# The tail of a fused conditioning and ternary-FFN kernel: gelu and last quarter by halves, a new order of the last matmuls, and second units at other pairs

## The chip, the core and the metric

The kernel runs on one core of a Trainium2 chip. The metric is device time in microseconds (us): 963.6 us is the median of four runs before the change (963.25 to 963.78). One more execution was recorded by the hardware profiler. It took 963.3 us, its span from the first to the last instruction is 961.5 us, and every time "at" some microsecond below counts from the start of that span. The engines are PE (TensorE, matmuls; PEld is its weight load), DVE (VectorE), ACT (ScalarE), POOL (GpSimd) and SP (SyncE, which only issues DMAs here).

## What is computed

Cut to what matters, the reference is

```python
w = weights[conditions]                      # one 64x64 matrix for each of 128 samples
c = einsum('bct,bcd->bdt', x, w)             # x: 128 x 64 x 512
h = gelu(c @ ternarize(W1).T + b1)           # 512 -> 2048
y = h @ ternarize(W2).T + b2                 # 2048 -> 512
scale = max(abs(y)) / 7 + 1e-8               # one scale for the whole tensor
out = x + clip(round(y / scale), -7, 7) * scale
```

ternarize replaces a weight matrix by alpha times a matrix of -1, 0 and 1.

## The kernel before, in words

The samples are worked in 16 blocks (n = 0 to 15) of 8 samples, which is 4 pairs of samples or 512 rows of 512 numbers. The hidden dimension is worked in 16 chunks (hc = 0 to 15) of 128. Every float32 activation is carried as two parts: a high part (k = 0, float32r) and a low part (k = 1, float16, what the high part lost). A chunk's hidden values are computed by layer 1, go through gelu, are split into the two parts, and layer 2 then adds their products with W2 into four accumulators `ypsum[n][j]`, j = 0 to 3, one for each quarter of the block's 512 rows, 128 x 512 float32, one PSUM bank each. The profile calls these accumulators py.

From block 2 on, chunks are worked in pairs by `pair(n, k)` and `seven(n, k, ...)`, k = 0 to 7: chunks 2k and 2k + 1 come out of seven products instead of eight. The products land in the PSUM tiles xy and z; ACT copies and DVE adds gather them into two SBUF tiles ha and hb (the profile calls these ring or x_quarters). Then come, for each of the two chunks, gelu (`gelu7`, ACT), a scaling copy that makes the high part (`high7`, with `up`, ACT; the profile's h) and the low part (`low`, with `rest`, DVE; the profile's low_parts or low_last). Layer 2 runs one pair behind: the matmuls of pair k use the chunks of pair k - 1 (`before[0]`, `before[1]`). POOL casts the fp8 weights to float32r for the high parts: `widen7` for the seven products (buffers `w1f[0..3]`), `widen2` for layer 2 (buffers `w2f[hc % 2]`); the profile calls all of them wf. Low parts use the fp8 weights directly (w1t, w2t, sums).

In the last block the low-part matmuls of chunks 8 to 15 (`HELD` = 8) are held back until all pairs are done. They and the last chunks' high parts make the tail at the end of the listing, a list of (quarter j, chunk hc, part k) that is worked in order. After a quarter's last matmul come y (DVE: accumulator times alpha plus bias), quantization (ACT), the largest magnitude (DVE, ymax) and `last_x(j)` (DVE: x plus quantized y times the scale, then the store). After the last quarter `widened` and `largest_of` form the maximum over the last blocks.

The quantization of earlier blocks must not wait for the end. Blocks 0 to 11 give a known maximum, from which the scale is taken; at the very end the maximum of the other blocks (top_rest) is compared with it, and a branch redoes the output if it is larger. So during blocks 12 to 15 finished half-blocks, "units", are put out between the pairs: `next_steps` quantizes a unit (ACT), `next_out` adds x (DVE) and stores it (SP), one unit behind the quantization. After every second unit `ahead_x` loads the x (and for blocks 0 and 1 the kept y) of a block to come; the load of the last block's x is the last of these. A pair has one unit (at `behind(0)`) or none; at some pairs a second unit is put in, quantized at `behind(2)` and added at `behind(4)`. The line `second = ...` in `pair` says which: in the last block, pairs 0 and 3.

What sets the order: each engine runs its instructions in the order in which the program text issues them (`InOrder` keeps that order), and waits only where data or buffers ask for it. `seven` calls `behind(i)` at fixed places between its products, and `behind` puts in what belongs there (casts, units, gathers, results of the block before). In `seven`, `last` is true only for pair 7 of block 15; there the order of the gelus and scalings already differs: gelu and scaling of the first chunk stand ahead of the second chunk's. The results of a block (y out of the accumulators) are taken at the end of pair 0 and the start of pair 1 of the next block.

The profile puts nearly everything on line 36, the helper that issues, so instructions are told apart by their tiles.

Of the kernel before, what the change touches and what calls it, by code (L numbers as in the profile page):

```python
# [15 lines left out]
AF = mybir.ActivationFunctionType  # L16
ALU = mybir.AluOpType
AX = mybir.AxisListType
# [21 lines left out]
def tile_cond_ternary_ffn(  # L40
# [51 lines left out]
    def pair_of_pairs(h):  # L92
        return slice(h * PAIRS // 2, (h + 1) * PAIRS // 2)
# [155 lines left out]
    def flat(w):  # L249
        return w.rearrange("p a b -> p (a b)")  # L250
# [129 lines left out]
    def widen2(n, hc):  # L380
        if n == 0 and hc < NH - LAG:
            w = w2f[hc % 4]
        else:
            w = w2f[hc % 2]
        if n == 0:
            g, i = divmod(hc, GH)
            pool.tensor_copy(w, group1(terns2, g)[:, i * T : (i + 1) * T])
        else:
            pool.tensor_copy(w, w2t[:, hc])
        wide2[n, hc] = w  # L390
# [44 lines left out]
    def two_of(n, hc):  # L435

        if not low_parts:
            t = half.tile([P, 4, BLK], F16, tag="half", name="low_parts")
            low_parts.extend(t[:, i, :] for i in range(4))
        if n == NB - 1 and hc == HELD:  # L440
            t = big.tile([P, NH - HELD, BLK], F16, tag="big", name="low_last")
            low_parts[:] = [t[:, i, :] for i in range(NH - HELD)]
        high = quarter.tile([P, BLK], F32R, tag="quarter", name=f"h_{n}_{hc}")
        return high, low_parts[hc % len(low_parts)]
# [3 lines left out]
    def up(high, h):  # L448
        act.activation(high, h, AF.Copy, scale=UP)

    def rest(two, h):
        dve.scalar_tensor_tensor(two[1], h, UP, two[0], ALU.mult, ALU.subtract)

    def low(n, hc):

        open_low.pop((n, hc), lambda: None)()

    def layer2(n, hc, js=range(PAIRS), ks=(1, 0), ends=None):
        two = hidden[n, hc]
        w = wide2[n, hc], wide2[n, hc] if n == 0 else w2t[:, hc]  # L460
        begins, ends = ks[0], ks[-1] if ends is None else ends
        if n not in ypsum:
            ypsum[n] = [
                ps_y.tile([P, T], F32, tag=f"py{j}", name=f"py{j}_{n}") for j in range(PAIRS)
            ]
        for k in ks:
            for j in js:
                pe.matmul(
                    out=ypsum[n][j],
                    lhsT=two[k][:, j * P : (j + 1) * P],  # L470
                    rhs=w[k],
                    start=(hc == 0 and k == begins and ends != begins),
                    stop=(hc == NH - 1 and k == ends),
                    skip_group_check=True,
                )
# [176 lines left out]
    def behind(hc):  # L652
        if hc == 6:
            largest2(0)
        if 6 <= hc < 6 + NG - 1:
            largest2(hc - 5)
        if hc == 7:
            sign1(3)
        if hc == 8:
            signed1(3)  # L660
        if hc == 11:
            delta.extend(next(find))
            signed2(0)
        if hc == 12:
            for i in (1, 3):
                low(0, i)
            signed2(1)
        if hc in (13, 14):
            widen2(0, hc - 13)
# [135 lines left out]
    def seven(n, k, behind, before, last):  # L805

        xb, xt, xl = cond[n]
        b11, b21, b22 = [(xb[:, i : i + 2], xl[:, i : i + 2]) for i in (0, 2, 4)]
        t1, t2, t3, t4 = [(xt[:, i : i + 2], xl[:, i + 6 : i + 8]) for i in (0, 2, 4, 6)]
        x, y = extra["xy"] if k % 2 == 0 else extra["xy"][::-1]  # L810
        x, y = x[:, :HALF], y[:, :HALF]
        z = extra["z"]
        p4, p5 = z[:, :HALF], z[:, HALF:]

        def both(w, narrow):
            return w, narrow.rearrange("p (c h) -> p c h", c=2)

        s0, s1, s2, s3 = sums_of(k)
        w11, w12 = both(w1f[0][:, :2], a11[:, k]), both(w1f[0][:, 2:], a12[:, k])
        w22 = both(w1f[1][:, 2:], a22[:, k])  # L820
        u0, u1 = both(w1f[1][:, :2], s0), both(w1f[2][:, :2], s1)
        u2, u3 = both(w1f[2][:, 2:], s2), both(w1f[3][:, :2], s3)

        def tokens(t):

            return t.rearrange("p (j h d) -> p h j d", j=PAIRS, h=2)

        def turned(t):
            return t.rearrange("p (j d) -> p j d", j=PAIRS)

        def gelu7(i, h):
            act.activation(h, h, AF.Gelu, bias=b1t[:, 2 * k + i : 2 * k + i + 1], scale=alpha[1])

        def high7(i, h):
            hc = 2 * k + i
            hidden[n, hc] = two = two_of(n, hc)
            up(two[0], h)
            open_low[n, hc] = lambda: rest(two, h)

        ha, hb = hf[0], hf[1]  # L840
        if n == NB - 1 and k % 2 == 1:
            ha, hb = extra["x"][:, 0, :], extra["x"][:, 1, :]
        ha_2, hb_2 = tokens(ha), tokens(hb)
        behind(0)
        product(x, w11, b11, 0, first=True)
        product(p5, u0, t1, 0, first=True)
        product(p4, w22, t4, 0)
        product(x, w11, b11, 1, last=True)
        act.copy(ha_2[:, 0], turned(x))
        product(p5, u0, t1, 1, last=True)  # L850
        product(p4, w22, t4, 1, last=True)
        act.copy(hb_2, z.rearrange("p (h j d) -> p h j d", h=2, j=PAIRS))
        behind(1)
        product(y, w12, b21, 1, first=True)
        product(y, w12, b21, 0, last=True)
        dve.tensor_tensor(ha_2[:, 0], turned(y), ha_2[:, 0], ALU.add)
        product(x, u1, t2, 0)
        product(x, u1, t2, 1, last=True)
        act.copy(ha_2[:, 1], turned(x))
        behind(2)  # L860
        product(p5, u2, b22, 1)
        product(p5, u2, b22, 0, last=True)
        dve.tensor_tensor(ha_2[:, 1], turned(p5), ha_2[:, 1], ALU.add)
        behind(3)
        layer2(*before[0], (0, 1), (0,), ends=1)
        product(x, u3, t3, 0)
        product(x, u3, t3, 1, last=True)
        dve.tensor_tensor(
            hb_2, turned(x).unsqueeze(1).to_broadcast([P, 2, PAIRS, C]), hb_2, ALU.add
        )  # L870
        gelu7(0, ha)
        behind(4)
        if last:
            high7(0, ha)
            gelu7(1, hb)
        else:
            gelu7(1, hb)
            high7(0, ha)
        if n < NB - 1 or before[0][1] < HELD:
            layer2(*before[0], (0, 1), (1,), ends=1)  # L880
            layer2(*before[0], (2, 3), (1,), ends=0)
            layer2(*before[1], ks=(1,), ends=0)
        layer2(*before[0], (2, 3), (0,), ends=0)
        layer2(*before[1], ks=(0,), ends=0)
        high7(1, hb)
        for i in range(2):
            low(n, 2 * k + i)
        behind(6)
# [128 lines left out]
    def widened(top, name):  # L1017

        top1 = const.tile([P, 1], F32, name=f"top1_{name}")
        dve.tensor_reduce(top1, top.rearrange("p n j -> p (n j)"), AX.X, ALU.max)  # L1020
        dve.tensor_copy(ones_f, top1.to_broadcast([P, P]))
        return ones_f
# [6 lines left out]
    def pair(n, k):  # L1029
# [11 lines left out]
        def behind(i):  # L1041
            if i == 0 and n >= KNOWN:
                if n == KNOWN and k < 2:
                    fetch_x(order[k])
                if k != 1 and (n > KNOWN or k > PAIRS - 1) and not (final and k > LAST):
                    next_steps()
                    next_out(True)
            second = n >= KNOWN and k in ((0, 3) if final else (0, NH // 2 - 1) if n > KNOWN else (NH // 2 - 1,))
            if i == 3 and n == KNOWN and k == PAIRS - 1:
                largest_of(tops_known.pop(), top_known, ps_c, "pc")  # L1050
                steps_of(scale, inverse, top_known)
# [80 lines left out]
    assert done[1] == len(units)  # L1132
    widen2(*steps[-1])
    pool.drain()
    lows = [(hc, 1) for hc in range(HELD, NH - 1)]
    rest_of = [(NH - 2, 0), (NH - 1, 0), (NH - 1, 1)]
    whole = lows + [(NH - 1, 1), (NH - 1, 0), (NH - 2, 0)]
    tail = [(0, *t) for t in lows + rest_of] + [(1, *t) for t in whole]
    tail += [(2, *t) for t in whole[::-1]] + [(3, *t) for t in whole]
    for i, (j, hc, k) in enumerate(tail):  # L1140
        final = all(j != t[0] for t in tail[i + 1 :])
        layer2(n, hc, [j], (k,), k if final else 1 - k)
        if not final:
            continue
        y = last[:, j, :]
        dve.scalar_tensor_tensor(y, ypsum[n][j], alpha[3], b2b, ALU.mult, ALU.add)
        act.activation(quant[:, j, :], y, AF.Identity, scale=inverse)
        dve.tensor_reduce(
            ymax[:, n, j : j + 1], y, AX.X, ALU.max, apply_absolute_value=True
        )  # L1150
        if j == PAIRS - 1:
            wide = widened(ymax[:, KNOWN:], "rest")
        last_x(j)
    top_rest = const.tile([P, 1], F32, name="top_rest")
    largest_of(wide, top_rest, ps_h, "ph")
# [74 lines left out]
```

## Time and profile before

| what | value |
|---|---|
| median of 4 runs | 963.6 us (963.25 to 963.78) |
| the profiled execution | 963.3 us, span 961.5 us |
| PE busy | 950.1 us, 99% of the span |
| DVE, POOL, ACT busy | 708.6, 706.3, 637.0 us |
| last pair's first product | 940.58 us |
| the six layer-2 matmuls at the end of the last pair | from 944.24 us |
| first matmul of the tail's list | 945.70 us |
| first y of the tail | 948.18 us |
| end of PE's last layer-2 matmul | 954.7 us |
| start of the last add of x | 956.82 us |
| end of the final comparison | 957.96 us |

The page of a profile begins with busy times of the engines and ends with groups of instructions; the groups give engine, operation, output and inputs by name, shapes, count, busy time, mean duration of one in ns, and after a bar the idle time of the engine just before them with what ended it. The chain follows the work that ended last back to the start: start, duration, engine and tile. A timeline row gives start, duration, engine, operation and, in brackets, the idle time before it. Instructions of one engine can overlap a little, so the distance between two starts is often shorter than a duration; a matmul of 512 columns has a row of about 0.4 us but follows the one before it by about 0.22 us.

### The profile page before, as it was taken

How to read it: one execution, taken by the hardware profiler on the slowest of the kernel's cores; microseconds unless marked ns; L12 is line 12 of the kernel's file. 1: busy time of each engine (PE TensorE's matmuls, PEld its weight loads, DVE VectorE, ACT ScalarE, POOL GpSimd, SP SyncE). 2: the span in 40 equal slices, each digit the busy share in tenths (PEclk: the TensorE clock that was granted, in tenths of full speed). 3: DMA queues.
4: the chain of work that ended last, by engine and by line, in shares of the span. 5: the costliest groups of instructions: out<-in, count | busy, mean ns of one | idle time of the engine just before them, and what ended most of it. 6: DMA issues, size and time to landing. Idle time of an engine off the chain costs nothing.

```text
span 961.5 us, 17574 instructions
## 1 busy us (share of the span) xinstructions
PE 950.1 (99%) x6072; PEld 739.5 (77%) x6072; DVE 708.6 (74%) x1239; ACT 637.0 (66%) x1148; POOL 706.3 (73%) x1060
## 2 busy tenths in 40 slices
PE   8999999999999999999999999999999999999997
PEld 4687667888788788788878778788878878878784
DVE  7999766666676766666676676666667798888986
ACT  7995445656656666665666656666565777878784
POOL 5866867677686776767767686776767879788872
PEclk9999999999999999999999999999999999999999
DMA  9201011110111100111020111100131184574751
GB/s 358 104 23 47 14 33 49 28 66 15 35 49 34 59 25 25 50 43 49 25 70 15 34 50 33 59 23 27 49 121 60 46 301 177 184 244 165 279 203 61
DMA packets 33195, 80.11 MB, mean 83 GB/s; under 512 B 3792, under 2 KB 3792, under 8 KB 30160
## 3 DMA queue, kind: packets, MB, share of 16 engines
q1 hardware_dynamic: 31056, 76.86, 22.9%
q0 software_dynamic: 2048, 2.10, 0.8%
q8 instruction: 49, 0.80, 0.4%
q14 instruction: 42, 0.34, 0.1%
HBM read 46.44 MB, written 32.51 MB: 82 GB/s over the span
## 4 chain that ended last, share of the span: by engine, by line
PE 96%; POOL 1%; DVE 1%; DMA 1%; issue 0%; ACT 0%; ACTq 0%; POOLq 0%
PE py L36 47%; PE xy L36 22%; PE z L36 16%; PE ph L36 6%; PE pc L36 6%; POOL wg L36 1%; DMA wg<-in_L_cond_weights,rows 1%; DVE xt L36 0%; DVE y_last L36 0%; POOL wf L36 0%; ACT diag L36 0%; DMA first<-in_itok_B 0%; POOL diag L36 0%; PE number L36 0%; DVE y L36 0%
## 5 line engine op out<-in xcount | busy, mean ns | idle before, releaser
L36 PE MATMUL py<-wf,h 128*128 128x512 f32 x1088 | 316.5, 416 | 0.7 <-DVE y L36 0.6
L36 POOL CAST wf<-w2t 128x512 fp32r<-128x512 fp8e4 x240 | 230.0, 979 | 105.2 <-PE py L36 102.2
L36 POOL CAST wf<-sums 128x256 fp32r<-128x256 fp8e4 (+1 forms) x336 | 183.2, 551 | 86.0 <-PE xy L36 82.4
L36 DVE SCALAR_TENSOR_TENSOR low_parts<-ring,h 128x512 f16<-128x512 f32 x228 | 202.5, 926 | 39.3 <-ACT h L36 39.3
L36 PEld LDWEIGHTS py<-wf,h 128*128 128x128 f32 x1088 | 196.6, 189 | 45.1 <-POOL wf L36 0.8
L36 PE MATMUL py<-w2t,low_parts 128*128 128x512 fp8e4 x920 | 218.6, 379 | 0.0
L36 ACT ACTIVATE ring<-ring,b1t,alpha_up 128x512 f32<-128x512 f32 x216 | 175.2, 818 | 58.8 <-DVE ring L36 53.9
L36 DVE TENSOR_TENSOR ring<-xy,ring 128x256 f32<-128x256 f32 x216 | 119.8, 555 | 119.2 <-PE xy L36 119.2
L36 ACT COPY ring<-xy 128x256 f32<-128x256 f32 x216 | 80.5, 373 | 171.6 <-PE xy L36 171.1
L36 PEld LDWEIGHTS <-low_parts 128*128 128x128 f16 x920 | 89.7, 98 | 84.4 <-issue 0.3
L36 ACT ACTIVATE h<-ring 128x512 fp32r<-128x512 f32 x232 | 133.9, 626 | 0.6
L36 POOL CAST wf<-w1t 128x256 fp32r<-128x256 fp8e4 (+1 forms) x240 | 131.3, 563 | 2.5 <-PE xy L36 0.3
L36 PE MATMUL xy<-xb,wf 128*128 128x256 f32 x448 | 98.8, 302 | 0.0
L36 PE MATMUL xy<-xt,wf 128*128 128x256 f32 x448 | 88.1, 277 | 0.1
L36 PE MATMUL xy<-xl,sums 128*128 128x256 f16 x448 | 87.9, 278 | 0.0
L36 PE MATMUL xy<-xl,w1t 128*128 128x256 f16 x448 | 86.8, 275 | 0.0
L36 PE MATMUL z<-xl,sums 128*128 128x256 f16 x448 | 85.6, 273 | 0.0
L36 PEld LDWEIGHTS xy<-xt,wf 128*128 128x128 f32 x448 | 76.2, 188 | 10.2 <-issue 0.2
L36 PEld LDWEIGHTS xy<-xb,wf 128*128 128x128 f32 x448 | 75.9, 189 | 10.2
L36 PEld LDWEIGHTS <-sums 128*128 128x128 fp8e4 x896 | 69.3, 97 | 14.7
L36 POOL DMA_INDIRECT wg<-in_L_cond_weights,rows x64 | 64.0, 999 | 18.2 <-issue 8.6
L36 PEld LDWEIGHTS <-w1t 128*128 128x128 fp8e4 x736 | 61.6, 98 | 18.0 <-issue 4.3
(134 smaller groups left out, 1349.7 us busy)
## 6 DMA issues: line engine op xcount, KB each, us to landing
xt<-in_x SPq DMA_DIRECT2D x36, 512.0 KB
y_dram<-y SPq DMA_DIRECT2D x15, 1024.0 KB
out<-xt SPq DMA_DIRECT2D x30, 512.0 KB
x_quarters<-in_x SPq DMA_DIRECT2D x56, 256.0 KB
nat<-in_L_ffn_W SPq DMA_DIRECT2D x6, 1024.0 KB
y_back<-y_dram SPq DMA_DIRECT2D x2, 1024.0 KB
nat<-in_L_ffn_W SPq DMA_DIRECT2D x3, 512.0 KB
wg<-in_L_cond_weights,rows POOLq DMA_INDIRECT x64, 2.5
```

What stands on the lines that cost most here:

```text
L36: return lambda *args, **kw: self._tc.keep_in_program_order(make(*args, **kw))
```

## The change

There are four edits.

1. In the last pair of the last block (`last` in `seven`), the add that completes hb is made in two halves of its columns, and gelu, scaling and low part of the second chunk are made for 256 columns at a time. The function then returns: the six layer-2 matmuls that stood at its end (chunk 12 for quarters 2 and 3, chunk 13 for all four) move into the tail.
2. The tail's list has a new order. Quarter 0 comes first, with the low parts of chunks 8 to 13 in front, then 13 high, 14 high, 14 low, 15 high, 15 low. Quarters 1 and 2 follow with 11 and 12 matmuls. Quarter 3 is worked in two column halves of its output: 12 matmuls of 256 columns, then y, quantization and maximum of these 256 columns, then the same for the other 256. The last add of x still takes all 512 columns. The second half's maximum goes into a slot of ymax that belongs to block 11, and the final reduction reads 20 values instead of 16.
3. `widen2` puts the last two chunks' weights into `w1f[0]` and `w1f[1]`, since the buffers `w2f` now stay in use until the tail.
4. In the last block the second units stand at pairs 3 and 4 instead of pairs 0 and 3.

```diff
--- before.py
+++ after.py
@@ -380,6 +380,8 @@
     def widen2(n, hc):
         if n == 0 and hc < NH - LAG:
             w = w2f[hc % 4]
+        elif n == NB - 1 and hc >= NH - 2:
+            w = flat(w1f[hc - NH + 2])
         else:
             w = w2f[hc % 2]
         if n == 0:
@@ -455,7 +457,7 @@
 
         open_low.pop((n, hc), lambda: None)()
 
-    def layer2(n, hc, js=range(PAIRS), ks=(1, 0), ends=None):
+    def layer2(n, hc, js=range(PAIRS), ks=(1, 0), ends=None, cols=slice(0, T)):
         two = hidden[n, hc]
         w = wide2[n, hc], wide2[n, hc] if n == 0 else w2t[:, hc]
         begins, ends = ks[0], ks[-1] if ends is None else ends
@@ -466,9 +468,9 @@
         for k in ks:
             for j in js:
                 pe.matmul(
-                    out=ypsum[n][j],
+                    out=ypsum[n][j][:, cols],
                     lhsT=two[k][:, j * P : (j + 1) * P],
-                    rhs=w[k],
+                    rhs=w[k][:, cols],
                     start=(hc == 0 and k == begins and ends != begins),
                     stop=(hc == NH - 1 and k == ends),
                     skip_group_check=True,
@@ -865,17 +867,24 @@
         layer2(*before[0], (0, 1), (0,), ends=1)
         product(x, u3, t3, 0)
         product(x, u3, t3, 1, last=True)
-        dve.tensor_tensor(
-            hb_2, turned(x).unsqueeze(1).to_broadcast([P, 2, PAIRS, C]), hb_2, ALU.add
-        )
+        for js in [pair_of_pairs(h) for h in range(2)] if last else [slice(0, PAIRS)]:
+            t = hb_2[:, :, js]
+            added = turned(x)[:, js].unsqueeze(1).to_broadcast(list(t.shape))
+            dve.tensor_tensor(t, added, t, ALU.add)
         gelu7(0, ha)
         behind(4)
         if last:
             high7(0, ha)
-            gelu7(1, hb)
-        else:
-            gelu7(1, hb)
-            high7(0, ha)
+            low(n, 2 * k)
+            hidden[n, 2 * k + 1] = two = two_of(n, 2 * k + 1)
+            for part in halves:
+                gelu7(1, hb[:, part])
+                up(two[0][:, part], hb[:, part])
+                rest([t[:, part] for t in two], hb[:, part])
+            behind(6)
+            return
+        gelu7(1, hb)
+        high7(0, ha)
         if n < NB - 1 or before[0][1] < HELD:
             layer2(*before[0], (0, 1), (1,), ends=1)
             layer2(*before[0], (2, 3), (1,), ends=0)
@@ -1045,7 +1054,7 @@
                 if k != 1 and (n > KNOWN or k > PAIRS - 1) and not (final and k > LAST):
                     next_steps()
                     next_out(True)
-            second = n >= KNOWN and k in ((0, 3) if final else (0, NH // 2 - 1) if n > KNOWN else (NH // 2 - 1,))
+            second = n >= KNOWN and k in ((3, 4) if final else (0, NH // 2 - 1) if n > KNOWN else (NH // 2 - 1,))
             if i == 3 and n == KNOWN and k == PAIRS - 1:
                 largest_of(tops_known.pop(), top_known, ps_c, "pc")
                 steps_of(scale, inverse, top_known)
@@ -1132,24 +1141,30 @@
     assert done[1] == len(units)
     widen2(*steps[-1])
     pool.drain()
-    lows = [(hc, 1) for hc in range(HELD, NH - 1)]
-    rest_of = [(NH - 2, 0), (NH - 1, 0), (NH - 1, 1)]
-    whole = lows + [(NH - 1, 1), (NH - 1, 0), (NH - 2, 0)]
-    tail = [(0, *t) for t in lows + rest_of] + [(1, *t) for t in whole]
-    tail += [(2, *t) for t in whole[::-1]] + [(3, *t) for t in whole]
-    for i, (j, hc, k) in enumerate(tail):
-        final = all(j != t[0] for t in tail[i + 1 :])
-        layer2(n, hc, [j], (k,), k if final else 1 - k)
-        if not final:
-            continue
-        y = last[:, j, :]
-        dve.scalar_tensor_tensor(y, ypsum[n][j], alpha[3], b2b, ALU.mult, ALU.add)
-        act.activation(quant[:, j, :], y, AF.Identity, scale=inverse)
-        dve.tensor_reduce(
-            ymax[:, n, j : j + 1], y, AX.X, ALU.max, apply_absolute_value=True
-        )
+    a, b, c, d = range(NH - 4, NH)
+    lows = [(hc, 1) for hc in range(HELD, b + 1)]
+    tail = [(0, *t) for t in lows + [(b, 0), (c, 0), (c, 1), (d, 0), (d, 1)]]
+    tail += [(1, *t) for t in [(d, 1), (c, 1)] + lows + [(b, 0), (c, 0), (d, 0)]]
+    tail += [(2, *t) for t in [(d, 0), (c, 0), (b, 0), (a, 0)] + lows + [(c, 1), (d, 1)]]
+    parts_of = {j: [slice(0, T)] for j in range(PAIRS - 1)}
+    parts_of[PAIRS - 1] = slice(0, HALF), slice(HALF, T)
+    for j in range(PAIRS):
+        group = [t[1:] for t in tail if t[0] == j]
         if j == PAIRS - 1:
-            wide = widened(ymax[:, KNOWN:], "rest")
+            group = [(d, 1), (c, 1)] + lows + [(hc, 0) for hc in (a, b, c, d)]
+        for i, part in enumerate(parts_of[j]):
+            for hc, k in group:
+                final = (hc, k) == group[-1]
+                layer2(n, hc, [j], (k,), k if final else 1 - k, part)
+            y, steps_y = last[:, j, part], quant[:, j, part]
+            dve.scalar_tensor_tensor(
+                y, ypsum[n][j][:, part], alpha[3], b2b[:, part], ALU.mult, ALU.add
+            )
+            act.activation(steps_y, y, AF.Identity, scale=inverse)
+            top = ymax[:, n, j : j + 1] if i == 0 else ymax[:, KNOWN - 1, :1]
+            dve.tensor_reduce(top, y, AX.X, ALU.max, apply_absolute_value=True)
+        if j == PAIRS - 1:
+            wide = widened(ymax[:, KNOWN - 1 :], "rest")
         last_x(j)
     top_rest = const.tile([P, 1], F32, name="top_rest")
     largest_of(wide, top_rest, ps_h, "ph")
```

## The prediction

> **What bounds the kernel now.** I read the page first (busy time, chain), then the waits, the chain of the last 60 us and the timeline of each engine there. On the page TensorE is the bound:
>
> ```profile
> PE 950.1 (99%) x6072; PEld 739.5 (77%) x6072; DVE 708.6 (74%) x1239; ACT 637.0 (66%) x1148; POOL 706.3 (73%) x1060
> ...
> PE 96%; POOL 1%; DVE 1%; DMA 1%; issue 0%; ACT 0%; ACTq 0%; POOLq 0%
> ...
> L36 PE MATMUL py<-wf,h 128*128 128x512 f32 x1088 | 316.5, 416 | 0.7 <-DVE y L36 0.6
> ```
>
> PE is 99% busy and makes 96% of the chain, so an edit counts only where PE waits or after its last matmul. The third line says where PE waits inside the blocks: once, for DVE's y. The chain puts that at 905.2 us, between pairs 0 and 1 of the last block:
>
> ```profile
> 900.48 0.70 DVE ring L36
> ...
> 901.20 0.82 ACT ring L36
> 902.02 1.04 ACT h L36 x2
> ...
> 904.99 0.75 DVE y L36
> 905.74 0.04 issue
> 905.78 0.51 PE py L36
> ```
>
> PE hands over the last product, DVE adds it, ACT does the second gelu and both scalings, DVE the two low parts and two y (the four reads of the old accumulators), and only then may PE write accumulators again. Pair 1 lasts 8.03 us (901.66 to 909.69), pair 2 lasts 7.09 and pair 3 6.81: the wait costs 1.2 us, and its wake in pair 2 another 0.3.
>
> At the end the chain is no longer PE's. From 948.18 on DVE repeats y, maximum, wait for ACT's quantization, x:
>
> ```profile
> 950.45 0.74 DVE L36 SCALAR_TENSOR_TENSOR y_last<-py,alpha_up,b2b 128x512 f32<-128x512 f32 x1
> 951.23 0.69 DVE L36 TENSOR_REDUCE ymax<-y_last 128x1 f32<-128x512 f32 x1
> 952.04 0.75 DVE L36 SCALAR_TENSOR_TENSOR xt<-diag,scale,xt 128x512 f32<-128x512 int8 x1
> 952.71 0.75 DVE L36 SCALAR_TENSOR_TENSOR y_last<-py,alpha_up,b2b 128x512 f32<-128x512 f32 x1
> ...
> 956.82 0.74 DVE L36 SCALAR_TENSOR_TENSOR xt<-diag,scale,xt 128x512 f32<-128x512 int8 x1
> ```
>
> y starts at 948.18, 950.45, 952.71 and 954.97: a period of 2.26 us, that is DVE's own loop, against 10 matmuls of about 0.222 = 2.22 us on PE. The last x starts at 956.82; what follows (x, store, comparison, end) takes 4.7 us to the span's end and moves with it. I therefore price the tail by the start of the last x.
>
> **The change, part by part.**
>
> *Second units.* Removed from pair 0: a quantization (ACT, 899.26, 1.15 us) and a scaled add with its store (DVE, 901.08, 1.29 us). They lie beside the chain above, not in it: ACT's second gelu waits for DVE's add at 901.17 and that for PE at 900.45; DVE is then idle 0.19 us waiting for ACT before the first low part. What can shrink is only contention: the low parts there take 0.82 and 1.09 us against 0.69 without POOL work (at 945.63), and the POOL cast that ran beside the add took 1.61 us against 0.62. So the bounds are 0 and -0.45 us (0.82 + 1.09 - 2 x 0.69 = 0.53, less some overlap of starts). POOL's next casts move up into the same low parts, and the mean low part is 0.93 us, so I take the near end, -0.1. Pair 4 receives them: DVE has 1.40 us idle there (before 929.58), the add goes in at 928.15; ACT's quantization (1.13) starts at about 926.48 and delays the second gelu from 928.21 to about 928.28. What these feed PE needs at 933.2, 3 us later, so cost 0; pair 3 carries two units already and runs in 6.81 us without a wait. On SP's queue the load of block 14's x moves from 902.8 to about 913 (used at 931) and the last block's x from 919.7 to about 922.7 (used at 949.8); stores of the moved unit follow. All with over 10 us of cover; at about 400 GB/s (the 905 us stretch) a 1 MB load takes 2.6 us.
>
> *First quarter in front.* Six high-part matmuls leave their place at 944.24 (1.36 us) and return among the quarters; 46 matmuls of 512 columns remain in sum. Quarter 0 can start its low parts at about 944.33: six (1.33), one high (0.23) to 945.89, high 14 to 946.11, low 14 waits for DVE (945.63 + 0.69), to 946.59, high 15 to 946.82, low 15 waits for its half.
>
> *Halves of gelu, scaling, low part.* Two more instructions each on ACT and DVE. A 256-wide gelu costs between 0.41 (half of 0.81) and 0.60 (0.81 less 0.21, as the ACT copy goes from 0.59 at 512 to 0.37 at 256); the scaling 0.31 to 0.42; the DVE low part 0.42 (the 256-wide add's row) to 0.48. From 945.51 this gives the first low half at 946.8 to 947.1 and the second at 947.5 to 948.0. DVE's first y stands behind the second half in its queue: 947.45 to 947.95, against 948.18. The add in halves (2 x 0.42 for 0.69) is covered by ACT, busy with the first gelu and scaling until 945.60. The last two weight casts go to first-layer buffers that are free after 942.5, so POOL no longer waits for PE until 945.08: no cost, over 2 us of cover.
>
> Then PE: quarter 0 done at 947.04 to 947.31, quarter 1 (11 x 0.2225) at 949.5 to 949.76, quarter 2 (12) at 952.16 to 952.43; a matmul's result is read about 0.2 us later, so y of quarter 2 starts at 952.38 to 952.63 (before 952.71).
>
> *Last quarter by column halves.* This is the term that decides. Matmuls of 256 columns run at 0.11 to 0.12 us (2 in 0.23, 4 in 0.46 in the chain), so a half of 12 takes 1.37 us and PE loses only 0.05. But both halves lie in one accumulator, and DVE reads the first while PE would write the second. Does the program let them overlap? The nearest rows are condition7's:
>
> ```profile
> L36 DVE TENSOR_TENSOR x_quarters<-x_quarters,pc 128x128 f32<-128x128 f32 x56 | 16.2, 289 | 31.3 <-ACT xb L36 31.3
> ```
>
> This DVE add needs only pc and the copy that ACT makes first, yet all 56 times it waits for ACT's two later casts xb, which merely read other columns of pc (in one case: copy 886.77 for 0.27, casts until 887.48, add at 887.51). So accesses of two engines to one accumulator bank are ordered even at different columns, and reads too. I take it that PE's second half waits for DVE's first read. The Trainium skill, "PSUM — Partial Sum Buffer", section "PSUM bank collisions raise a hardware error", states the same for the chip, and speaks against this change: two engines on one bank and quadrant collide even at disjoint columns, and one guards by bank, not by address. By a rule of addresses the sum would be the second rival's, by this one the forecast's; no run here shows a collision.
>
> With the wait: the first half's y starts one DVE period after quarter 2's (+2.27, since it is queued behind quarter 2's x), at 954.65 to 954.9, though PE had it ready at about 953.7. It takes 0.48 (0.75 less 0.27, the step of the add from 0.69 to 0.42). PE starts the second half at 955.2 to 955.4 and delivers at 956.75 to 957.0 (1.37 + 0.2). Then y 0.51, maximum 0.45, reduction 0.20, copy 0.14: the last x starts at 958.05 to 958.3, against 956.82: **+1.2 to +1.5, taken +1.35**. Behind the waiting PE instruction stand only the other 11 half matmuls and the last transpose; DVE's second y, ACT's last quantization and the last store wait for them.
>
> **Sum.** 963.3 (the profiled execution, span 961.5) - 0.1 + 1.35 = 964.55. The median shown is 963.6, 0.3 above that execution, so I forecast **964.8** there; own range with the bounds (-0.45 to 0, +1.2 to +1.5) 964.3 to 965.2.
>
> **Rivals.**
> 1. *The halves overlap freely.* Then DVE bounds the end: from the first half's y (954.65 to 954.9) y 0.51, maximum (next start after 0.35), y 0.51, maximum 0.45, reduction 0.20, copy 0.14 make 2.16 to the last x, against 1.85 now: 956.8 to 957.05, +0.1. With -0.1: 963.6. For it: the regions don't overlap. Against: the row of 56 waits. 8%.
> 2. *The stall at 905 goes altogether* (-1.2 and -0.3), with the bank's wait: 963.6 + 1.35 - 1.5 = 963.45. For it: ACT and DVE are the engines PE waits for there, and both are relieved. Against: DVE's 0.19 us of idle before the low part shows that the unit was not in the way. 7%; with free halves too it would be 962.2.
> 3. *Slower: TensorE's clock drops in the new wait.* PE stands about 1.5 us before the second half; at half the rate that half takes 1.4 us more: 964.8 + 1.4 = 966.2. It decides if the granted clock falls after a gap of that length. Against: after 2.33 us of idle the transpose at 957 still ran in a microsecond with 1.00 granted; only from 958 on the clock is down (0.73). 4%.
>
> The forecast holds 75%, another 6% goes to some other wait of DVE or ACT in the tail that adds up to 1 us. A measurement can tell about 0.2%, 1.9 us, from no change: faster lies below 961.7, slower above 965.5. Faster 2%: only rival 2 with more that I don't see. Slower 9%: rival 3, half of the 6%, and the forecast's upper tail. Same 89%. The range reaches down to the first two rivals and to just under the slower bound: 963.4 to 965.5.
>
> **What will show it.** Right: a new PE wait of about 1.5 us on DVE y_last near 954 to 955; the last x some 1.35 us later against the start of pair 7; first y 0.2 to 0.7 us earlier; pair 1 within 0.4 us of 8.0; pair 4 at 6.8 without a PE wait. Wrong: second-half matmuls starting before the first half's y has ended (rival 1), pair 1 at about 6.9 (rival 2), a clock under 1.00 near 956 (rival 3), a PE wait in pairs 4 or 5.

## The result and the profile after

The changed kernel takes 964.64 us (median of 40 runs, 964.39 to 966.05) against 963.35 us for the kernel before (60 runs, 963.19 to 963.96). The ratio is 1.0014 with a 95% interval of 1.0009 to 1.0018: 1.3 us slower, a loss that is clear of noise and smaller than the 0.2% that the prediction took as the least that a measurement can tell from no change. The profiled execution took 964.58 us, its span is 962.8 us.

The page after hardly differs from that of before; the wait of PE between the blocks is a little shorter (0.5 for 0.7):

```profile
PE 950.7 (99%) x6084; PEld 741.0 (77%) x6084; DVE 708.9 (74%) x1243; ACT 637.8 (66%) x1151; POOL 705.0 (73%) x1060
...
L36 PE MATMUL py<-wf,h 128*128 128x512 f32 x1092 | 316.7, 415 | 0.5 <-DVE y L36 0.4
```

The loss is in the last 10 us. The timeline there (start, duration, engine, operation, shapes, and in brackets the idle time before):

```profile
952.42 0.75 DVE L36 SCALAR_TENSOR_TENSOR y_last<-py,alpha_up,b2b 128x512 f32<-128x512 f32 x1
...
953.01 0.72 PE L36 MATMUL py<-wf,h 128*128 128x256 f32 x4
...
954.02 0.75 DVE L36 SCALAR_TENSOR_TENSOR xt<-diag,scale,xt 128x512 f32<-128x512 int8 x1
954.69 0.48 DVE L36 SCALAR_TENSOR_TENSOR y_last<-py,alpha_up,b2b 128x256 f32<-128x256 f32 x1
955.20 0.42 DVE L36 TENSOR_REDUCE ymax<-y_last 128x1 f32<-128x256 f32 x1
955.22 1.03 PE L36 MATMUL py<-w2t,low_last 128*128 128x256 fp8e4 x8 [1.49 <-DVE y_last L36]
...
956.01 0.72 PE L36 MATMUL py<-wf,h 128*128 128x256 f32 x4
956.77 0.48 DVE L36 SCALAR_TENSOR_TENSOR y_last<-py,alpha_up,b2b 128x256 f32<-128x256 f32 x1 [1.15 <-PE py L36]
...
958.09 0.74 DVE L36 SCALAR_TENSOR_TENSOR xt<-diag,scale,xt 128x512 f32<-128x512 int8 x1
```

PE ends the first half's matmuls at 953.7 and stands until 955.22, just after DVE's first half y (954.69 to 955.17). That y could not start earlier, because quarter 2's add of x (954.02) is ahead of it in DVE's queue. Then DVE in turn stands 1.15 us for the second half's matmuls. The last add of x starts at 958.09 instead of 956.82, although pair 7 starts 0.14 us earlier (940.44 for 940.58).

### The profile page after: what moved, and what is told of

It reads as the page before. It is cut to its first block, busy times and chain, and to the rows that moved or that the text cites. A ratio compares the mean times of both kernels' runs of the same rounds, so it can differ in the third digit from the quotient of the medians.

```text
span 962.8 us, 17604 instructions
## 1 busy us (share of the span) xinstructions
PE 950.7 (99%) x6084; PEld 741.0 (77%) x6084; DVE 708.9 (74%) x1243; ACT 637.8 (66%) x1151; POOL 705.0 (73%) x1060
## 4 chain that ended last, share of the span: by engine, by line
PE 96%; DVE 2%; DMA 1%; ACT 0%; POOL 0%; issue 0%; SPq 0%; DVEq 0%; ACTq 0%
PE py L36 47%; PE xy L36 22%; PE z L36 16%; PE pc L36 6%; PE ph L36 6%; DMA nat<-in_L_ffn_W 1%; DVE top L36 1%; DVE y_last L36 0%; POOL wf L36 0%; DVE xt L36 0%; DVE y L36 0%; PE number L36 0%; ACT x_quarters L36 0%; SPq L36 0%; ACT diag L36 0%
```

## The experiments

The theory is the prediction's: the two column halves lie in one PSUM bank, PE's second half is made to wait for DVE's read of the first, and DVE's loop delays that read. The rivals: the extra instructions of the halves are the loss, or the new order of the tail with its gelu halves is. The first four kernels ran on one chip beside the kernel before (963.23 us), the second four likewise (963.26 us); each median is of 11 runs (33 of the kernel before), the interval is that of the ratio. The intervals are about 0.9 us to either side, so differences of a few tenths are read from the traces, by the start of the last add of x. Code is cut to what matters.

**halves_only.** To the kernel before, only the column halves are added; its list keeps its order:

```diff
-        layer2(n, hc, [j], (k,), k if final else 1 - k)
+        for i, part in enumerate(parts_of[j]):   # quarter 3: two halves
+            layer2(n, hc, [j], (k,), k if final else 1 - k, part)
```

> The kernel before with the column halves of the last quarter alone (old order of the matmuls, gelu whole, units at pairs 0 and 3). Theory (PE's second half waits for DVE's first y, since both halves lie in one bank): in the changed kernel the first half's y starts 2.08 us ahead of the second half's, and that 1.32 us ahead of the last x; with the first half's y at 954.97 as before, the last x starts at 958.4 against 956.82, so +1.5 us on the kernel before, with one PE wait of 1.4 to 1.6 us on y_last. Rival (the halves overlap, only the extra instructions cost): +0.3 us and no PE wait. Rival (the loss comes from the new order and the gelu halves): 0.

Measured: 964.46 us, ratio 1.0013 (1.0004 to 1.0022), +1.2 us. This edit alone makes the loss. The wait is there, and longer than in the changed kernel (1.87 for 1.49 us), as quarter 3's first half has 10 matmuls here and not 12, so PE is done with it 0.24 us earlier, and DVE's y starts 0.14 us later. From the timeline:

```profile
953.01 0.48 PE L36 MATMUL py<-wf,h 128*128 128x256 f32 x2
...
954.83 0.48 DVE L36 SCALAR_TENSOR_TENSOR y_last<-py,alpha_up,b2b 128x256 f32<-128x256 f32 x1
...
955.36 1.03 PE L36 MATMUL py<-w2t,low_last 128*128 128x256 fp8e4 x8 [1.87 <-DVE y_last L36]
...
956.67 0.48 DVE L36 SCALAR_TENSOR_TENSOR y_last<-py,alpha_up,b2b 128x256 f32<-128x256 f32 x1 [0.91 <-PE py L36]
...
957.99 0.74 DVE L36 SCALAR_TENSOR_TENSOR xt<-diag,scale,xt 128x512 f32<-128x512 int8 x1
```

My +1.5 was 0.3 too high: it took the time between the two y (2.08 us) from the changed kernel, whose halves have 12 matmuls; in the old order quarter 3 has 10, and that time is 1.84 us.

**whole_last.** The changed kernel with one line undone:

```diff
-    parts_of[PAIRS - 1] = slice(0, HALF), slice(HALF, T)
+    parts_of[PAIRS - 1] = [slice(0, T)]
```

> The changed kernel with its last quarter whole again, all other edits kept. Theory: the PE wait on y_last goes; y of quarter 2 started at 952.42, twelve matmuls at 0.2225 us make y of quarter 3 ready at 955.1, the last x starts 1.85 us later at 956.95, so +0.1 us on the kernel before and 1.2 us below the changed one. Rival (order or gelu halves cost the 1.3 us): about +1.3 us on the kernel before, like the changed kernel.

Measured: 963.43 us, ratio 1.0003 (0.9993 to 1.0012). The loss is gone but for 0.2 us, so order and gelu halves don't make it. PE has no wait on y_last; instead DVE waits for PE's last matmuls, and the last add of x starts at 956.96 (expected 956.95):

```profile
955.10 0.75 DVE L36 SCALAR_TENSOR_TENSOR y_last<-py,alpha_up,b2b 128x512 f32<-128x512 f32 x1 [0.30 <-PE py L36]
...
956.96 0.74 DVE L36 SCALAR_TENSOR_TENSOR xt<-diag,scale,xt 128x512 f32<-128x512 int8 x1
```

**evac_halves.** The halves' instructions on DVE and ACT without the halves' matmuls:

```diff
-            for hc, k in group:
+            for hc, k in group if i == 0 else []:
                 final = (hc, k) == group[-1]
-                layer2(n, hc, [j], (k,), k if final else 1 - k, part)
+                layer2(n, hc, [j], (k,), k if final else 1 - k)
```

> The changed kernel with the last quarter's 12 matmuls whole, but y, quantization and maximum still by column halves: the extra instructions without the wait of PE. Theory: first y at 955.1 as with a whole last quarter, last x 2.16 us later at 957.25, so +0.4 us on the kernel before, 0.3 above the whole last quarter. Rival (the extra instructions on DVE and ACT are the loss): +1.3 us, like the changed kernel.

Measured: 963.70 us, ratio 1.0006 (0.9996 to 1.0015). PE has no wait on y_last:

```profile
955.03 0.48 DVE L36 SCALAR_TENSOR_TENSOR y_last<-py,alpha_up,b2b 128x256 f32<-128x256 f32 x1 [0.30 <-PE py L36]
...
955.89 0.47 DVE L36 SCALAR_TENSOR_TENSOR y_last<-py,alpha_up,b2b 128x256 f32<-128x256 f32 x1
...
957.20 0.74 DVE L36 SCALAR_TENSOR_TENSOR xt<-diag,scale,xt 128x512 f32<-128x512 int8 x1
```

The last add of x starts 2.17 us after the first y, against 1.86 in whole_last (the medians differ by 0.27). So the extra instructions cost 0.3 us, and not 1.3.

**own_bank.** The second half's matmuls go to a tile in a bank of its own, and what the old bank holds of these columns is read ahead, at the start of pair 7. In the two lower pieces only the second half changes; the first half keeps the old lines:

```diff
+            if i == 0 and leaves:    # behind(0) of pair 7
+                dve.scalar_tensor_tensor(last[:, 3, HALF:], ypsum[n][3][:, HALF:],
+                    alpha[3], b2b[:, HALF:], ALU.mult, ALU.add)
...
-                layer2(n, hc, [j], (k,), k if final else 1 - k, part)
+                pe.matmul(out=own, lhsT=hidden[n, hc][k][:, j * P : (j + 1) * P],
+                    rhs=w[:, part], start=((hc, k) == group[0]), stop=final)
...
-            dve.scalar_tensor_tensor(y, ypsum[n][j][:, part], alpha[3], b2b[:, part], ALU.mult, ALU.add)
+            dve.scalar_tensor_tensor(y, own, alpha[3], y, ALU.mult, ALU.add)
```

> The changed kernel, but the second column half adds its 12 matmuls in a PSUM bank of its own; what the old bank holds of these columns is read by one more DVE instruction (0.48 us) at the start of pair 7, where DVE has time. Theory: PE goes on with the second half at once, no PE wait on y_last; DVE's loop bounds the end and the last x starts 2.16 us after the first half's y at 954.7, at 956.85, so about 0 against the kernel before and 1.2 us below the changed kernel. Rival (PE waits for something else, or the price is the halves' instructions): no change against the changed kernel, +1.3 us on the kernel before.

Measured: 963.34 us, ratio 1.0002 (0.9993 to 1.0011). The same 24 half matmuls, one more DVE instruction, and no wait: PE goes from the old bank to the new one while DVE is busy elsewhere.

```profile
953.62 1.05 PE L36 MATMUL y_own<-w2t,low_last 128*128 128x256 fp8e4 x8
...
954.42 0.72 PE L36 MATMUL y_own<-wf,h 128*128 128x256 f32 x4
954.74 0.48 DVE L36 SCALAR_TENSOR_TENSOR y_last<-py,alpha_up,b2b 128x256 f32<-128x256 f32 x1
...
955.59 0.47 DVE L36 SCALAR_TENSOR_TENSOR y_last<-y_own,alpha_up,y_last 128x256 f32<-128x256 f32 x1
...
956.90 0.75 DVE L36 SCALAR_TENSOR_TENSOR xt<-diag,scale,xt 128x512 f32<-128x512 int8 x1
```

The profiled executions begin the last pair at slightly different times. Counted from the start of pair 7 to the start of the last add of x, the five kernels and the one before compare like this:

| kernel | pair 7 | last add of x | between |
|---|---|---|---|
| before | 940.58 | 956.82 | 16.24 us |
| changed | 940.44 | 958.09 | 17.65 us |
| halves_only | 940.44 | 957.99 | 17.55 us |
| whole_last | 940.46 | 956.96 | 16.50 us |
| evac_halves | 940.39 | 957.20 | 16.81 us |
| own_bank | 940.48 | 956.90 | 16.42 us |

So 1.23 us (17.65 less 16.42) go when the halves no longer share a bank. The new order with its gelu halves costs 0.26 us by itself (16.50 less 16.24); these two edits were not tried apart. One thing stays open: every accumulator is one tile that fills one bank, and own_bank's second half has both a tile and a bank of its own. The runs can't tell an order kept by bank from one kept by whole tile.

The Trainium skill, "PSUM — Partial Sum Buffer", section "Summary: rules for kernel authors", gives the remedy: to read PSUM while matmuls run, use a different bank. Here that is worth 964.64 - 963.35 less 963.34 - 963.23, 1.2 us. But it only brings the time back to that of the kernel before: with the halves free, DVE's loop bounds the tail (954.74 plus 2.16 us of DVE work to the last add of x, where a whole quarter needs 1.85).

The second group asks what stands behind the stall at 905 us and what the moved units are worth.

**units_only.** The kernel before with the units' line alone:

```diff
-k in ((0, 3) if final
+k in ((3, 4) if final
```

> The kernel before with the second units at pairs 3 and 4 of the last block and nothing else changed. Theory (the unit was hidden beside the chain; only contention on the low parts shrinks): pair 1 of the last block gets 0.1 us shorter, -0.1 us on the kernel before. Rival (the unit holds PE up at 905): pair 1 falls to 6.9 us and the time by 1.2 to 1.5 us.

Measured: 963.06 us, ratio 0.9998 (0.9989 to 1.0007); pair 1 lasts 7.90 us (901.54 to 909.44), 0.13 less. A gain of 0.1 to 0.2 us, which the interval can't tell from none but the pair's length shows. A pair starts with its first product:

```profile
901.54 0.40 PE L36 MATMUL xy<-xb,wf 128*128 128x256 f32 x2
...
909.44 0.40 PE L36 MATMUL xy<-xb,wf 128*128 128x256 f32 x2
```

**early_y_oldtail.** As units_only, and in pair 0 of the last block the four y of the block before go ahead of the two low parts in DVE's queue:

```diff
         high7(1, hb)
+        behind(5)                # pair 0 of block 15: results(range(PAIRS))
         for i in range(2):
             low(n, 2 * k + i)
         behind(6)                # no longer results([0]) there,
                                  # nor results(1..3) in pair 1
```

> As units_only, and in pair 0 of the last block the four y of the block before are taken ahead of the pair's two low parts instead of behind them; the tail is that of the kernel before. Theory: the stall at 905 is DVE's queue order (two low parts that wait for ACT stand ahead of the y that PE waits for); DVE has 1.4 us idle there, y can start at 901.9, PE's wait for y goes (1.1 us), and part of it comes back in pair 2, since DVE's adds of pair 1 come only 0.6 us earlier: -0.6 to -1.3 us on the kernel before. Rival (the wait only moves to the low parts or to ACT): within 0.2 us of units_only.

Measured: 961.79 us, ratio 0.9985 (0.9976 to 0.9994), -1.5 us where -0.6 to -1.3 was expected: faster than both kernels, and 1.27 us below units_only. In the timeline after units_only, then after early_y_oldtail, DVE's long idle time has turned into the y:

```profile
902.46 1.69 DVE L36 SCALAR_TENSOR_TENSOR low_parts<-ring,h 128x512 f16<-128x512 f32 x2 [1.41 <-ACT h L36]
...
904.07 2.72 DVE L36 SCALAR_TENSOR_TENSOR y<-py,alpha_up,b2b 128x512 f32<-128x512 f32 x4
...
904.95 1.07 PE L36 MATMUL py<-wf,h 128*128 128x512 f32 x2 [0.45 <-DVE y L36]
```

```profile
901.02 2.73 DVE L36 SCALAR_TENSOR_TENSOR y<-py,alpha_up,b2b 128x512 f32<-128x512 f32 x4
...
903.66 1.69 DVE L36 SCALAR_TENSOR_TENSOR low_parts<-ring,h 128x512 f16<-128x512 f32 x2
...
904.31 0.63 PE L36 MATMUL py<-wf,h 128*128 128x512 f32 x2
...
908.35 0.40 PE L36 MATMUL xy<-xb,wf 128*128 128x256 f32 x2
```

The first accumulator was done by 901.02, where its y now starts without a wait, and the other y follow without a gap; before, the y stood in the queue behind low parts that waited for ACT. With the y in front PE doesn't wait in these pairs: pairs 1 and 2 last 6.84 and 6.81 us (901.51, 908.35, 915.16). I had expected part of the gain to come back in pair 2; none did, since DVE's adds of pair 1 moved up by 1.4 us (905.28 for 906.70), not by 0.6.

**early_y.** The same with the changed kernel's tail, its last quarter whole.

> As early_y_oldtail, but with the changed kernel's tail, its last quarter whole. Theory: the two parts add up: whole_last stood at +0.2 on the kernel before, so -0.4 to -1.1 us on the kernel before. Rival: +0.2, like whole_last.

Measured: 962.05 us, ratio 0.9987 (0.9978 to 0.9996), -1.2 us, just past the 1.1 expected. The parts add up; the new order of the tail is 0.26 us behind the old one here too.

**early_y_units.** As early_y, with the second units back at pairs 0 and 3.

> As early_y, but with the second units back at pairs 0 and 3. Theory: the unit's add holds DVE until 902.4 there, so the early y start 0.5 us later and the low parts behind them too: 0.3 to 0.7 us above early_y. This tells if the units' move opened room that only another order of DVE's queue uses. Rival (the unit never matters): the same as early_y.

Measured: 962.91 us, ratio 0.9996 (0.9989 to 1.0005), 0.86 us above early_y, a little more than expected. The unit's add holds DVE until 902.4 and the low parts come late:

```profile
901.12 1.29 DVE L36 SCALAR_TENSOR_TENSOR xt<-y,scale,xt 128x1024 f32<-128x1024 int8 x1
...
902.33 2.71 DVE L36 SCALAR_TENSOR_TENSOR y<-py,alpha_up,b2b 128x512 f32<-128x512 f32 x4
...
904.97 1.48 DVE L36 SCALAR_TENSOR_TENSOR low_parts<-ring,h 128x512 f16<-128x512 f32 x2
...
905.70 0.55 PEld L36 LDWEIGHTS <-low_parts 128*128 128x128 f16 x4 [0.40 <-DVE low_parts L36]
```

PE's weight loads wait for low_parts, twice (0.40 and 0.26 us); pair 1 lasts 7.14 us (901.69 to 908.83) and pair 2, which waits for ACT once, 7.35. So the units' move is worth 0.1 to 0.2 us in the old order of DVE's queue and 0.9 in the new one; and without the move the new order saves only 0.6 us in pairs 1 and 2 (14.49 us for 15.12).

## Why the prediction was right, step by step

- **Second units, taken -0.1.** Right: pair 1 went from 8.03 to 7.89 us (901.69 to 909.58), pair 4 runs in 6.80 us (923.45 to 930.25) with its second unit and no PE wait, and units_only confirms the size. That the unit was in no one's way was true for this order of the queue only, as early_y_units shows; the 1.41 us of idle DVE that the move left ahead of the low parts was not used by the change.
- **First quarter in front, gelu by halves.** The first y came at 947.71 (947.45 to 947.95 predicted), quarter 2's at 952.42 (952.38 to 952.63). The half-width gelu took 0.59 us, the scaling 0.42, the low part 0.42: the upper ends of the first two bounds, so on ACT two halves cost 0.37 us more than a whole gelu (0.81). The first y's gain, 0.3 us after pair 7's shift, was more than eaten up. PE's weight loads wait twice in quarter 0 (0.48 and 0.21 us, for the low parts of chunks 14 and 15), and quarters 2 and 3 now have 12 matmuls each where the old list had 10: in whole_last one y follows the other by 2.26, 2.46 and 2.65 us, where DVE's own loop takes 2.26. So PE bounds the tail again, and whole_last's last add of x comes 0.26 us later than before, counted from pair 7.
- **Column halves, taken +1.35.** The step that decided, and right: the first half's y at 954.69 (954.65 to 954.9), a PE wait of 1.49 us (about 1.5), second half from 955.22, its y at 956.77 (956.75 to 957.0), last add of x at 958.09 (958.05 to 958.3).
- **Sum.** 964.55 for a profiled execution, 964.58 measured, and not by errors that cancel: the terms came to -0.14 (pair 1) and, from pair 7 on, +1.41. The upper end of its own range adds up to 965.1, not 965.2. The median of 964.8 was 0.16 high because the four runs shown lay 0.25 above the median of 60.
- **Rivals.** Free halves: refuted by the wait; own_bank, which makes them free, starts the last add of x at 956.90, as that rival priced it (956.8 to 957.05). The stall goes by the units' move: refuted by pair 1; the stall itself was real and needed another order in DVE's queue. The clock: it stayed at 1.00 in every microsecond from 953 to 958, through a PE gap of 1.49 us. The 0.73 that the prediction read "from 958 on" is a mean to the end of the span; in the kernel before, the microsecond from 958 still has 1.00 and the next 0.80.

The rows on which the prediction rested the column halves, those of condition7, it read not quite rightly. DVE's add, which waits 56 times for ACT's casts, reads `pc[:, :2, :C]`. Of the two casts the first reads `pc[:, :, :C]`, which includes these columns; only the second, `pc[:, 2:, C:]`, reads others. DVE goes on when the second has ended, and add and casts only read pc, so the conclusion holds, but for the second cast alone. In the kernel before:

```profile
886.77 0.27 ACT L36 COPY x_quarters<-pc 128x128 f32<-128x128 f32 x1 [0.48 <-PE pc L36]
886.93 0.55 ACT L36 CAST xb<-pc 128x256 fp32r<-128x256 f32 x2
...
887.51 0.29 DVE L36 TENSOR_TENSOR x_quarters<-x_quarters,pc 128x128 f32<-128x128 f32 x1 [0.34 <-ACT xb L36]
```

These rows are of ACT and DVE. That PE waits likewise was a step by analogy, which the changed kernel's own wait and own_bank bear out. Where the prediction gives the sum by a rule of addresses to "the second rival", the first is meant, in which the halves overlap.

Not tried: a kernel in which PE writes one column half of a bank while DVE reads the other without the wait. What the chip would do then, no run here shows.

## What to carry to other kernels

Cutting an accumulator's columns in two gave overlap of matmul and read here only when the halves lay in tiles in different PSUM banks; in one bank the second half's matmuls were put behind the first half's read, and behind whatever stood ahead of that read in the reader's queue. Before cutting an instruction in two, count the fixed part: here two halves of y cost 0.2 us more on DVE, and two halves of a gelu 0.4 on ACT. Before moving work between the parts of a tail, count what each part then holds: 12 matmuls in the last quarters instead of 10 made PE the bound there. And where PE waits for an engine, look at what stands ahead in that engine's queue: moving four reads ahead of two instructions that wait for a third engine saved 1.3 us with the units moved and 0.6 without, more than any edit of the change gained.

## What the runs showed of the hardware that was not expected

POOL's casts took longer beside some of DVE's instructions, and taking the unit out moved that instead of ending it. Before the change, beside the unit's add of 1.29 us, a cast of 128x512 took 1.61 us, against 0.62 at 909.08; without the add two such casts together took 1.33 us. The lines are of the kernel before, then of the changed one:

```profile
901.08 1.29 DVE L36 SCALAR_TENSOR_TENSOR xt<-y,scale,xt 128x1024 f32<-128x1024 int8 x1
901.24 1.61 POOL L36 CAST wf<-w2t 128x512 fp32r<-128x512 fp8e4 x1
```

```profile
901.27 1.33 POOL L36 CAST wf<-w2t 128x512 fp32r<-128x512 fp8e4 x2
...
902.60 1.69 DVE L36 SCALAR_TENSOR_TENSOR low_parts<-ring,h 128x512 f16<-128x512 f32 x2 [1.41 <-ACT h L36]
902.89 1.88 POOL L36 CAST wf<-w1t 128x256 fp32r<-128x256 fp8e4 x2
904.21 2.71 DVE L36 SCALAR_TENSOR_TENSOR y<-py,alpha_up,b2b 128x512 f32<-128x512 f32 x4
```

The two casts of 128x256 that follow then ran beside the low parts and took 1.88 us (0.96 before, at 904.62, beside the y), and the first y came only 0.12 us earlier (904.21 for 904.33). On ACT a gelu of half the width costs 0.59 us against 0.81, so 73% of the whole, where DVE's reads of PSUM fall to 64% (0.48 of 0.75).
